# Reordering the joints of a graph-layer kernel: messages two batches ahead, weight combination in portions, first loads of the last phase on the GpSimd queue

**Chip, cores, metric.** One core of one Trainium2 chip. The metric is device microseconds for one execution; several executions of each kernel are timed and the median is given. The kernel before takes 2006.34 us (three runs, 2004.92 to 2007.96).

## The reference

A pre-norm graph layer on x of 32 x 512 x 256, fp32, with one 512 x 512 adjacency per batch. Cut to what matters:

```python
h = jnp.maximum(_layernorm(x), 0.0)
# 1. two convolutions along the nodes (1 tap, 17 taps), each with a batch norm
c = relu(_bn(_conv1d(hT, conv1_w, 0)))
x_conv = relu(_bn(_conv1d(c, conv2_w, 8)) + hT)
# 2. messages along edges, weighted by a distance of 3 features per node
s = h @ w_se.T + b_se
A = jnp.exp(-dist(s)) * adj
x_nmp = A @ relu(h @ w_msg.T + b_msg)
# 3. a GRU cell over [x_conv, x_nmp] with state h
gi = concat([x_conv, x_nmp]) @ w_ih.T + b_ih ;  gh = h @ w_hh.T + b_hh
r, z = sigmoid(...), sigmoid(...) ;  n = tanh(gi_n + r * gh_n)
out = x + (1 - z) * n + z * h
```

## The kernel before

The 32 batches go in two groups of 16, in stages one after the other:
- *first part* of a group: layer norm, transposed h, first convolution, its windows taken to frequency space. In the first group TensorE also generates the second convolution's weights there ("steps").
- *node loop* of a group: message, distances, aggregate for each batch, interleaved with *products* (the second convolution in frequency space).
- *last phase*: pairs of batches; inverse transform, then the gates by a seven-product block scheme. It needs sums of weights (the *combination*: `wraw` to `wsum7`, stored, later loaded as `sw`) and sums of the operands `hp` (h), `np` (aggregate) and `cp` (convolution).

```python
def statistics(b):                      # VectorE, then one GpSimd power
    for c in range(NC):
        nc.vector.bn_stats(...); nc.vector.bn_aggr(...)
    nc.vector.tensor_scalar(rstd, mv[:, :, 1], LN_EPS, None, op0=ALU.add)
    nc.gpsimd.tensor_tensor(rstd, rstd, minus_half[:, :NC], op=ALU.pow)

def first_part(g, xf, between):
    ...
    for b in range(b0, b1):
        if b + 3 < b1: load_x(b + 3, nc.gpsimd)
        if b == b0:    conv1(b)
        if b + 2 < b1: statistics(b + 2)
        if b + 1 < b1: transpose_h(b + 1)
        if b + 2 < b1: normalise(b + 2)
        one, two = between(b - b0)
        ... # conv1(b), steps `one`, windows_to_freq(b - 1), steps `two`

def nodes(g, xf, last):
    load_nodes(b0); message(b0); features(b0); factors(b0)
    for b in range(b0, b1):
        affinity(b)
        if more: load_nodes(b + 1); message(b + 1); features(b + 1)
        ... # two products
        if more: factors(b + 1)
        aggregate(b); save_nmp(b); HT.pop(b)
        ... # remaining products

with phase("pw"):
    with phase("nodes"): nodes(0, xf, GB)
    with phase("first", "sums"):
        combine_weights()               # all three, ahead of the second first part
        first_part(1, xf, lambda i: ([], []))
    with phase("nodes"): nodes(1, xf, GB - 3)

# last phase, all on the sync queue
load_pair(0); sw = load_combined()
sums(HP[0], True); sums(NP[0], False); inverse(0); sums(CP[0], False)
for p in range(pairs): ...
```

In the traces below each engine works through its instructions in the order of its stream (at 560.11 the power comes only after all of the combination's operations from 554.02 on). So "ahead" and "behind" in this text mean places in one engine's stream.

## Time and profile before

| | before |
|---|---|
| median | 2006.34 us |
| profiled span | 2007.6 us |
| TensorE busy / idle | 1929.0 / 78.6 us |
| largest waits of TensorE in the joints | features in the node loops 15.8, normalised x 14.1, first load of the last phase 11.6, first load of the next group 4.6 |

The lines behind this are in the prediction below. How to read a timeline line: start, duration, engine, source line, operation, out<-in, shape, how many instructions, and in brackets the engine's idle time before it with what ended that. In a waits line the three numbers are total us, times, longest. A window row has its stretch, its length, the busy time of PE, PEld, DVE, ACT and POOL, TensorE's granted clock as a share of full speed, the DMA share (mean busy share of the 16 transfer engines) and GB/s. PE is TensorE's matmuls and PEld its weight loads, DVE is VectorE, ACT ScalarE, POOL GpSimd, and SPq the sync queue. Of the tile names, phT is the transposed x, px the windows in frequency space, psl and psr belong to the features, pn is the aggregate (in the last phase a gate), yt the stored result of the second convolution, which the inverse transform (pc from yt) reads.

### The profile page before, as it was taken

What the parts mean: (1) busy time and instruction counts of PE and PEld (TensorE: products, weight loads), DVE (VectorE), ACT (ScalarE), POOL (GpSimd) and SP (SyncE); (2) the same over time, 40 slices, a digit from 0 to 9 for tenths busy, and PEclk for the clock granted to TensorE, in tenths of its full rate; (3) what the DMA queues carried; (4) which work ended last, traced back from release to release, by engine and by line L of the source; (5) the groups of instructions that cost most, each with busy time, mean ns of one, the idle gap of its engine ahead of it and who ended that gap; (6) DMA issues with size and microseconds to landing.
All of it is one profiled execution on the core that took longest, in us unless ns stands there. A gap on an engine that the chain in (4) does not pass through costs nothing.

```text
span 2007.6 us, 21238 instructions
## 1 busy us (share of the span) xinstructions
PE 1929.0 (96%) x7328; PEld 1188.8 (59%) x7328; DVE 1158.1 (58%) x2197; ACT 546.3 (27%) x930; POOL 541.7 (27%) x544
## 2 busy tenths in 40 slices
PE   7998999999799999998799999999999999999997
PEld 5666667766598677775455455554555545555453
DVE  7774666666795566664234555445554455544555
ACT  2444333333144233332122112221122212222121
POOL 2330323333521334340413221222213222132210
PEclk9997999999899999998699999999999999999998
DMA  8997788787654879884804331334213442134301
GB/s 208 289 262 210 201 234 221 229 233 211 228 194 130 223 226 241 242 222 114 263 20 123 123 86 54 107 124 123 78 53 116 124 123 76 51 121 124 123 11 53
DMA packets 238506, 310.92 MB, mean 155 GB/s; under 512 B 13775, under 2 KB 188687, under 8 KB 237631
## 3 DMA queue, kind: packets, MB, share of 16 engines
q1 hardware_dynamic: 220991, 260.72, 45.7%
q10 hardware_dynamic: 12224, 31.86, 4.1%
q0 software_dynamic: 5184, 16.98, 3.2%
q8 instruction: 59, 0.97, 0.2%
q14 instruction: 48, 0.39, 0.1%
HBM read 202.62 MB, written 106.89 MB: 154 GB/s over the span
## 4 chain that ended last, share of the span: by engine, by line
PE 87%; DVE 6%; DMA 4%; issue 2%; ACT 1%; POOL 1%; SPq 0%; DVEq 0%; POOLq 0%; ACTq 0%
PE pg L492 29%; PE pn L492 14%; PE pn L398 11%; PE py L316 9%; PE pc L481 6%; PE pm L350 6%; PE pc L269 3%; PE px L283 2%; DMA wd<-wst 2%; PE pd L384 2%; PE po L615 1%; PE pw L214 1%; DVE x L245 1%; DVE stats L234 1%; PE phT L256 1%
## 5 line engine op out<-in xcount | busy, mean ns | idle before, releaser
L398 PE MATMUL pn<-A,msg 128*128 128x512 f32 x512 | 231.5, 605 | 3.8 <-DVE A L390 3.8
L492 PE MATMUL pg<-hp,sw 128*128 128x512 f32 x448 | 229.8, 595 | 0.0
L492 PE MATMUL pg<-np,sw 128*128 128x512 f32 x448 | 229.7, 594 | 0.0
L492 PE MATMUL pg<-cp,sw 128*128 128x512 f32 x448 | 229.2, 593 | 0.0
L470 POOL TENSOR_TENSOR hp<-hp 128x512 f32<-128x512 f32 x64 | 80.5, 1268 | 476.3 <-DMA hp<-hd 268.9
L398 PEld LDWEIGHTS pn<-A,msg 128*128 128x128 f32 x512 | 96.8, 195 | 116.4 <-issue 110.1
L470 POOL TENSOR_TENSOR cp<-cp 128x512 f32<-128x512 f32 x64 | 80.5, 1268 | 296.2 <-ACT cp L486 294.9
L507 ACT ACTIVATE rz<-rz,brz 128x512 f32<-128x512 f32 x96 | 69.2, 721 | 298.7 <-DVE rz L511 298.7
L492 PEld LDWEIGHTS pg<-cp,sw 128*128 128x128 f32 x448 | 85.4, 191 | 107.7 <-issue 107.5
L492 PEld LDWEIGHTS pg<-np,sw 128*128 128x128 f32 x448 | 85.4, 191 | 107.7 <-issue 107.0
L316 PE MATMUL py<-wt,both 128*128 128x256 f32 x624 | 147.5, 379 | 0.0
L308 POOL TENSOR_TENSOR both<-xf 128x256 f32<-128x256 f32 x78 | 58.9, 755 | 301.5 <-PE py L316 256.2
L350 PEld LDWEIGHTS pm<-wmsg,hT 128*128 128x128 f32 x512 | 124.3, 327 | 25.3 <-issue 22.0
L492 PEld LDWEIGHTS pg<-hp,sw 128*128 128x128 f32 x448 | 83.0, 191 | 92.6 <-issue 89.0
L389 DVE STREAM_TRANSPOSE at<-adj 128x512 f32<-128x512 f32 x128 | 134.7, 1086 | 1.8 <-DMA adj<-in_adj_dram 1.4
L350 PE MATMUL pm<-wmsg,hT 128*128 128x259 f32 x512 | 135.4, 419 | 0.0
L481 PEld LDWEIGHTS pc<-back,yt 120*128 120x128 f32 x1024 | 123.4, 201 | 20.0 <-DMA yt<-yd 12.8
L311 POOL TENSOR_TENSOR wsum<-wt 128x512 f32<-128x512 f32 x78 | 101.6, 1302 | 124.4 <-DMA wt<-wd 120.7
L400 DVE COPY nmp<-pn 128x512 f32<-128x512 f32 x64 | 44.3, 692 | 157.5 <-PE pn L398 157.5
L481 PE MATMUL pc<-back,yt 120*128 120x80 f32 (+1 forms) x1024 | 123.2, 284 | 11.8 <-DMA yt<-yd 11.6
L316 PEld LDWEIGHTS py<-wt,both 128*128 128x128 f32 x624 | 118.9, 191 | 25.2 <-issue 10.8
L269 PE MATMUL pc<-w,hT 128*128 128x256 f32 x512 | 121.0, 391 | 0.6 <-DVE hT L257 0.6
(110 smaller groups left out, 2964.5 us busy)
## 6 DMA issues: line engine op xcount, KB each, us to landing
wt<-wd SPq DMA_DIRECT2D x160, 256.0 KB, 5.6
adj<-in_adj_dram SPq DMA_DIRECT2D x128, 256.0 KB, 5.2
yd<-y ACTq DMA_DIRECT2D x80, 384.0 KB, 5.7
yt<-yd SPq DMA_DIRECT2D x64, 480.0 KB, 10.0
wd<-wst SPq DMA_DIRECT2D x64, 320.0 KB, 5.1
x<-in_x_dram SPq DMA_DIRECT2D x38, 512.0 KB, 5.5
hd<-hT SPq DMA_DIRECT2D x32, 512.0 KB, 4.1
hT<-hd SPq DMA_DIRECT2D x32, 512.0 KB, 3.5
```

The lines of the kernel that those rows point to most:

```text
L269: nc.tensor.matmul(p[:, j, :], HT[b][:, ic, c * P : (c + 1) * P], w1[:, ic, :], start=(ic == 0), stop=(ic == DC - 1))
L308: nc.gpsimd.tensor_tensor(both[:, 0], re, im, op=ALU.add)
L311: nc.gpsimd.tensor_tensor(wsum, wr, wi, op=ALU.add)
L316: nc.tensor.matmul(dst, v[:, ic, :], w[:, ic, :], start=(ic == 0), stop=(ic == DC - 1))
L350: nc.tensor.matmul(p[:, : D + NS], chunk(HT[b][:, ic, :], c), wmsg[:, ic, :], start=(ic == 0), stop=(ic == DC - 1))
L389: nc.vector.transpose(at.rearrange("p (j k) -> p j k", k=32), ADJ[b].rearrange("p j (q c) -> p c j q", c=NC)[:, mc])
L398: nc.tensor.matmul(p, MSG[b][:, mc, dc * P : (dc + 1) * P], A[b][:, mc, :], start=(mc == 0), stop=(mc == NC - 1))
L400: nc.vector.tensor_copy(NMP[b][:, dc, :], p)
L470: nc.gpsimd.tensor_tensor(t[:, dst, :], t[:, a, :], t[:, b, :], op=sub)
L481: nc.tensor.matmul(bk[:, t0:t1], YT[p][j * W + w][:, oc * P : (oc + 1) * P], back[:, u0 : u0 + t1 - t0], start=(w == 0), stop=(w == W - 1) ...
L492: nc.tensor.matmul(bk, sw[:, k, q, o, :], terms[k][q], start=(first and i == 0), stop=(i == len(ks) - 1), skip_group_check=True)
L507: nc.scalar.activation(rz[:, g, j, :], src, AF.Sigmoid, bias=brz[:, g : g + 1], scale=1.0)
```

## The change

The intent: keep TensorE busy where one stage ends and the next starts. Five parts:
1. The generated weights' steps are spread over 15 batches instead of 16, so that their last stores are done before the node loop.
2. The node loop sends messages two batches ahead and distances one ahead. It starts with the group's last batch, whose hT is kept in SBUF.
3. The combination moves from ahead of the second first part into it, one third after each of the batches 2, 6 and 10.
4. The first loads of the last phase go out on the GpSimd queue, while the node loop still runs; yt ahead of np; the combined weights in two portions, the first-needed first (the operands are renumbered for that).
5. In the last pair two of four blends run on GpSimd, and the first batch is finished ahead of the last blend; in every pair results are stored in halves. Further, in the second group, the second batch is normalised before the first is transposed.

```diff
 # weight steps
-                mine = spread(steps, b, GB)
-                return mine[::2], mine[1::2]
+                mine = spread(steps, b, GB - 1) if b < GB - 1 else []
+                return mine[:1], mine[1:]
 # node loop (begin(i): load hT if it isn't there, message, features)
+            todo = [b1 - 1] + list(range(g * GB, b1 - 1))
+            load_adj(todo[0])
+            begin(0)
+            factors(todo[0])
+            begin(1)
+            affinity(todo[0])
+            for i, b in enumerate(todo):
+                if more:
+                    load_adj(todo[i + 1])
+                    factors(todo[i + 1])
+                for u in mine[:1]:
+                    product(pools["pw"], g, u, xf)
+                begin(i + 2)
+                if more:
+                    affinity(todo[i + 1])
 ...                                     # a product, aggregate, save, products
 # combination
-                combine_weights()
+                def between(b):
+                    if b % 4 == 2 and b // 4 < K3:
+                        combine_weights(b // 4)
+                    return [], []
 # last phase
-        load_pair(0)
-        sw = load_combined()
-        sums(HP[0], True)
-        sums(NP[0], False)
+        load_pair(0, nc.gpsimd)
+        load_combined(sw, 0, 2)         # on the GpSimd queue
+        load_combined(sw, 2, 7)
         inverse(0)
-        sums(CP[0], False)
+        for t, keep in ((HP[0], True), (NP[0], False), (CP[0], False)):
+            sums(t, keep)
 # second group of the first part
-        transpose_h(b0)
+        if g == 0:
+            transpose_h(b0)
         statistics(b0 + 1)
         normalise(b0 + 1)
+        if g > 0:
+            transpose_h(b0)
 # last pair
+        if last:
+            blend(0, 0, nc.gpsimd)
+            blend(1, 1, nc.gpsimd)
+            blend(1, 0)
+            finish(p, 0)
+            blend(0, 1)
+            finish(p, 1)
```

(Cut: buffer counts of msg 2 to 3 and A 1 to 2, hT released after the message, order of loads within a pair, half stores.)

More of the change, by code (lines that the diff above doesn't have):

```diff
@@ L273, in conv1 @@
             nc.scalar.activation(h1, h1, AF.Relu)
-        del HT[b]
+        if b % GB != GB - 1:
+            del HT[b]
     def windows_to_freq(b, xf):
@@ L322, in product, with load_adj @@
         nc.scalar.dma_start(YD[g][:, 3 * u : 3 * u + 3, :], y)
-    def load_nodes(b):
-        load_h(b)
-        ADJ[b] = pools["nodes"].tile([P, N // 32, P], FP, tag="adj", name=f"adj_{b}")
+    def load_adj(b):
+        ADJ[b] = pools["nodes"].tile([P, N // 32, P], FP, tag="adj", name=f"adj_{b}", bufs=1)
         rows = adj[b].rearrange("(j r) (g m) -> g r j m", r=32, g=4)
@@ L340, in message @@
     def message(b):
-        MSG[b] = pools["nodes"].tile([P, NC, D], FP, tag="msg", name=f"msg_{b}", bufs=2)
+        MSG[b] = pools["nodes"].tile([P, NC, D], FP, tag="msg", name=f"msg_{b}", bufs=3)
         ST[b] = pools["nodes"].tile([P, 2, NC, NS], FP, tag="st", name=f"st_{b}", bufs=2)
@@ L354, in message @@
             nc.scalar.activation(m, m, AF.Relu)
+        del HT[b]
     def features(b):
@@ L377, in affinity @@
     def affinity(b):
-        A[b] = pools["nodes"].tile([P, NC, N], FP, tag="A", name=f"A_{b}")
+        A[b] = pools["nodes"].tile([P, NC, N], FP, tag="A", name=f"A_{b}", bufs=2)
         sl, sr = SL.pop(b), SR.pop(b)
@@ L404, in save_nmp @@
         nc.sync.dma_start(ND[b], NMP.pop(b))
-    A11, A12, S4, A22, S1, S2, S3 = range(7)
+    Q1, Q6, Q2, Q7, Q5, Q4, Q3 = range(7)
     B11, B12, B21, B22 = range(4)
-    def combine_weights():
-        sources = [w_hhT, w_ihT[D:], w_ihT[:D]]
-        for k, src in enumerate(sources):
-            w = pools["sums"].tile([P, DC, G], FP, tag="wraw", name=f"wraw_{k}")
-            nc.sync.dma_start(w, src.rearrange("(c p) o -> p c o", p=P))
-            w = w.rearrange("p c (g i o) -> p c g i o", i=2, o=P)
-            a11, a21, a12, a22 = w[:, 0, :, 0], w[:, 0, :, 1], w[:, 1, :, 0], w[:, 1, :, 1]
-            t = pools["sums"].tile([P, 7, 3, P], FP, tag="wsum7", name=f"wsum7_{k}")
-            for dst, a in ((A11, a11), (A12, a12), (A22, a22)):
-                nc.gpsimd.tensor_copy(t[:, dst], a)
-            nc.gpsimd.tensor_tensor(t[:, S1], a21, a22, op=ALU.add)
-            nc.gpsimd.tensor_tensor(t[:, S2], t[:, S1], a11, op=ALU.subtract)
-            nc.gpsimd.tensor_tensor(t[:, S3], a11, a21, op=ALU.subtract)
-            nc.gpsimd.tensor_tensor(t[:, S4], a12, t[:, S2], op=ALU.subtract)
-            nc.sync.dma_start(WS[k], t)
@@ L432, in load_combined, with combine_weights @@
-    def load_combined():
-        sw = pools["sw"].tile([P, K3, 7, 3, P], FP, name="sw")
+    def combine_weights(k):
+        src = [w_hhT, w_ihT[D:], w_ihT[:D]][k]
+        w = pools["sums"].tile([P, DC, G], FP, tag="wraw", name=f"wraw_{k}")
+        nc.sync.dma_start(w, src.rearrange("(c p) o -> p c o", p=P))
+        w = w.rearrange("p c (g i o) -> p c g i o", i=2, o=P)
+        a11, a21, a12, a22 = w[:, 0, :, 0], w[:, 0, :, 1], w[:, 1, :, 0], w[:, 1, :, 1]
+        t = pools["sums"].tile([P, 7, 3, P], FP, tag="wsum7", name=f"wsum7_{k}")
+        for dst, a in ((Q1, a11), (Q2, a12), (Q4, a22)):
+            nc.gpsimd.tensor_copy(t[:, dst], a)
+        nc.gpsimd.tensor_tensor(t[:, Q5], a21, a22, op=ALU.add)
+        nc.gpsimd.tensor_tensor(t[:, Q6], t[:, Q5], a11, op=ALU.subtract)
+        nc.gpsimd.tensor_tensor(t[:, Q7], a11, a21, op=ALU.subtract)
+        nc.gpsimd.tensor_tensor(t[:, Q3], a12, t[:, Q6], op=ALU.subtract)
+        nc.sync.dma_start(WS[k], t)
@@ L434, in load_combined, with load_pair @@
+    def load_combined(sw, q0, q1):
         for k in range(K3):
-            nc.sync.dma_start(sw[:, k], WS[k])
-        return sw
-    def load_pair(p):
+            nc.gpsimd.dma_start(sw[:, k, q0:q1], WS[k][:, q0:q1])
+    def load_pair(p, queue=nc.sync):
+        NP[p] = pools["ops"].tile([P, 7, N], FP, tag="np", name=f"np_{p}")
         HP[p] = pools["ops"].tile([P, 8, N], FP, tag="hp", name=f"hp_{p}")
-        NP[p] = pools["ops"].tile([P, 7, N], FP, tag="np", name=f"np_{p}")
         YT[p] = []
@@ L443, in load_pair @@
             b = 2 * p + j
-            nc.sync.dma_start(HP[p][:, j:4:2], HD[b])
-            nc.sync.dma_start(NP[p][:, j:4:2], ND[b])
-        for j in range(2):
-            b = 2 * p + j
+            queue.dma_start(HP[p][:, j:4:2], HD[b])
             g, w0 = b // GB, (b % GB) * W
@@ L451, in load_pair @@
                 w = w0 + k * (W // 2)
-                nc.sync.dma_start(t, YD[g][w : w + W // 2].rearrange("w r d -> r w d"))
+                queue.dma_start(t, YD[g][w : w + W // 2].rearrange("w r d -> r w d"))
                 YT[p] += [t[:, i, :] for i in range(W // 2)]
+        for j in range(2):
+            queue.dma_start(NP[p][:, j:4:2], ND[2 * p + j])
     def load_pair_x(p):
@@ L463, in operands @@
         t3 = 7 if keep else B12
-        return [t[:, i, :] for i in (B11, B21, B22, 6, 4, 5, t3)]
+        return [t[:, i, :] for i in (B11, 5, B21, t3, 4, 6, B22)]
     def sums(t, keep):
@@ L493, in into @@
                              skip_group_check=True)
-    Q1, Q2, Q3, Q4, Q5, Q6, Q7 = range(7)
     def temp(role, name):
@@ L542, in gates_rz, with gate_n @@
             result(b3[o], u2[o], o, 0, 1)
-    def gate_n(p, terms):
+    def gate_n(p, terms, last):
         rz, o = RZ[p], 2
@@ L567, in closing, with blend @@
             nc.scalar.activation(n, n, AF.Tanh, bias=b_in[:, i : i + 1], scale=1.0)
-        def blend(i, j):
+        def blend(i, j, engine=nc.vector):
             n, d = nt[:, i, j, :], rz[:, i, j, :]
-            nc.vector.tensor_sub(d, HP[p][:, 2 * i + j, :], n)
-            nc.vector.tensor_mul(d, d, rz[:, DC + i, j, :])
-            nc.vector.tensor_add(n, n, d)
+            engine.tensor_tensor(d, HP[p][:, 2 * i + j, :], n, op=ALU.subtract)
+            engine.tensor_tensor(d, d, rz[:, DC + i, j, :], op=mul)
+            engine.tensor_tensor(n, n, d, op=add)
         x1 = [bank(f"pn1_{p}_{k}") for k in range(2)]
@@ L602, in gate_n @@
         closing(x3[1], 0, 1)
-        for i, j in ((0, 0), (1, 1), (1, 0), (0, 1)):
-            blend(i, j)
+        if last:
[5 more added lines that the diff above has]
+            finish(p, 1)
+        else:
+            for i, j in ((0, 0), (1, 1), (1, 0), (0, 1)):
+                blend(i, j)
     def finish(p, j):
@@ L617, in finish @@
             nc.vector.tensor_add(xo, xo, bk)
-        nc.sync.dma_start(out[b].rearrange("(c p) d -> p c d", p=P), xb)
+            nc.sync.dma_start(out[b].rearrange("(c p) d -> p c d", p=P)[:, c0 : c0 + h], xo)
     def spread(todo, i, n):
@@ L690, in nodes, with begin @@
         def nodes(g, xf, last):
-            b0, b1 = g * GB, (g + 1) * GB
+            b1 = (g + 1) * GB
+            todo = [b1 - 1] + list(range(g * GB, b1 - 1))
             units = list(range(UNITS))
-            load_nodes(b0)
-            message(b0)
-            features(b0)
-            factors(b0)
-            for b in range(b0, b1):
-                mine = spread(units, b - b0, last) if b - b0 < last else []
-                more = b + 1 < b1
-                affinity(b)
+            def begin(i):
+                if i < GB:
+                    if todo[i] not in HT:
+                        load_h(todo[i])
+                    message(todo[i])
+                    features(todo[i])
+            load_adj(todo[0])
[4 more added lines that the diff above has]
+            for i, b in enumerate(todo):
+                mine = spread(units, i, last) if i < last else []
+                more = i + 1 < GB
                 if more:
-                    load_nodes(b + 1)
-                    message(b + 1)
-                    features(b + 1)
-                for u in mine[:2]:
+                    load_adj(todo[i + 1])
+                    factors(todo[i + 1])
+                for u in mine[:1]:
                     product(pools["pw"], g, u, xf)
+                begin(i + 2)
                 if more:
-                    factors(b + 1)
+                    affinity(todo[i + 1])
+                for u in mine[1:2]:
+                    product(pools["pw"], g, u, xf)
                 aggregate(b)
                 save_nmp(b)
-                HT.pop(b)
                 for u in mine[2:]:
@@ L718, in gnn_layer @@
             with phase("first", "sums"):
-                combine_weights()
+                def between(b):
+                    if b % 4 == 2 and b // 4 < K3:
+                        combine_weights(b // 4)
+                    return [], []
                 xf = freq_tile(1)
                 with tc.manual_schedule():
-                    first_part(1, xf, lambda i: ([], []))
+                    first_part(1, xf, between)
             with phase("nodes"):
@@ L729, in gnn_layer @@
         pairs = B // 2
-        load_pair(0)
-        sw = load_combined()
-        sums(HP[0], True)
-        sums(NP[0], False)
+        sw = pools["sw"].tile([P, K3, 7, 3, P], FP, name="sw")
+        load_pair(0, nc.gpsimd)
+        load_combined(sw, 0, 2)
+        load_combined(sw, 2, 7)
         inverse(0)
-        sums(CP[0], False)
+        for t, keep in ((HP[0], True), (NP[0], False), (CP[0], False)):
+            sums(t, keep)
         for p in range(pairs):
@@ L754, in gnn_layer @@
                 sums(CP[p + 1], False)
-            gate_n(p, terms)
-        for j in range(2):
-            finish(pairs - 1, j)
+            gate_n(p, terms, not more)
 def kernel(**inputs):
```

## The prediction

> **What bounds the kernel now.** I began with the page's busy shares and its 40 slices.
>
> ```profile
> PE 1929.0 (96%) x7328; PEld 1188.8 (59%) x7328; DVE 1158.1 (58%) x2197; ACT 546.3 (27%) x930; POOL 541.7 (27%) x544
> ```
>
> TensorE bounds it: 1929.0 of 2007.6 us busy. The static comparison of the two kernels gives the same instructions and shapes on every engine, in another order. So only two things can be won: TensorE's idle time (78.6 us), and the stretching of its work at half clock. To see where they lie I cut the span by stage (columns: stretch, length, busy time of PE, PEld, DVE, ACT, POOL with instruction counts, granted clock, DMA share, GB/s).
>
> ```profile
> 0.00:150.00 150.00, 136.67 (x760) 95.09 (x760) 115.11 (x310) 64.21 (x140) 45.07 (x67) 0.99 0.93 253
> 150.00:230.00 80.00, 67.64 (x295) 48.88 (x292) 43.59 (x105) 29.74 (x58) 15.42 (x16) 0.85 0.73 206
> 230.00:500.00 270.00, 270.00 (x1079) 187.49 (x1078) 177.42 (x344) 88.47 (x146) 93.43 (x103) 1.00 0.80 224
> 500.00:540.00 40.00, 26.17 (x111) 19.63 (x110) 29.59 (x65) 4.34 (x9) 19.90 (x24) 0.79 0.67 235
> 540.00:630.00 90.00, 89.77 (x550) 83.52 (x549) 73.71 (x199) 36.30 (x86) 23.89 (x28) 1.00 0.49 172
> 630.00:680.00 50.00, 45.37 (x177) 32.22 (x177) 25.01 (x62) 16.52 (x27) 13.54 (x15) 0.93 0.68 176
> 910.00:964.00 54.00, 44.09 (x140) 25.51 (x138) 25.74 (x56) 13.85 (x22) 0.00 (x0) 0.87 0.36 93
> 964.00:992.00 28.00, 16.52 (x67) 14.91 (x68) 3.46 (x5) 2.89 (x4) 11.90 (x10) 0.55 0.98 319
> 992.00:1990.00 998.00, 998.00 (x3214) 514.62 (x3212) 505.89 (x745) 215.57 (x316) 229.05 (x183) 1.00 0.31 93
> ```
>
> The loops' steady states (230 to 500, 680 to 910) and the last phase from 992 are 100% busy at full clock: nothing to win. The loss sits in the joints. Counting idle time plus busy time x (1 - clock):
> - first part to node loop, 150 to 230: 12.4 + 10.1 = 22.5 us
> - node loop to second first part, 500 to 540: 13.8 + 5.5 = 19.3
> - second first part to second node loop, 630 to 680: 4.6 + 3.2 = 7.8
> - end of that loop, 910 to 964: 9.9 + 5.7 = 15.6
> - start of the last phase, 964 to 992: 11.5 + 7.4 = 18.9
>
> Sum 84 us. The start and the final blends (some 28 us more) are hardly touched.
>
> TensorE's waits name the causes (total, times, longest):
>
> ```profile
> PE psl L370 <- DVE fr L364: 15.8, 6, 4.1
> PE phT L256 <- DVE x L245: 14.1, 6, 6.3
> PE pc L481 <- DMA yt<-yd: 11.6, 1, 11.6
> PE px L283 <- DVE hT L257: 4.6, 1, 4.6
> ```
>
> The first is the ends of the node loop, where the chain message, features, factors, affinity of one batch has no other batch's work beside it. The other three I followed in the timeline:
>
> ```profile
> 151.01 0.43 DVE L234 BATCH_NORM_STATS2 stats<-x 128x6 f32<-128x256 f32 x1 [5.26 <-DMA x<-in_x_dram]
> 513.52 0.99 POOL L429 TENSOR_TENSOR wsum<-wraw,wsum 128x384 f32<-128x384 f32 x1
> 514.47 1.02 POOL L239 TENSOR_TENSOR rstd<-rstd,minus_half 128x4 f32<-128x4 f32 x1
> 515.52 3.19 DVE L245 TENSOR_SCALAR x<-x,mv,rstd 128x256 f32<-128x256 f32 x4 [4.91 <-POOL rstd L239]
> 543.42 1.40 POOL L425 COPY wsum<-wraw 128x384 f32<-128x384 f32 x3 [2.95 <-DMA wraw<-in_w_ihT_dram]
> 975.33 2.00 PE L481 MATMUL pc<-back,yt 120*128 120x72 f32 x8 [11.60 <-DMA yt<-yd]
> 989.49 2.01 PE L492 MATMUL pg<-hp,sw 128*128 128x512 f32 x2
> ```
>
> At 151 statistics of the next group's x, hoisted into this phase, wait for a load and hold VectorE's queue. At 514 the power that gives rstd sits behind the weight combination on GpSimd; the normalise behind it then takes 3.19 us instead of 1.4. At 975 TensorE has waited 11.6 us for the first load of the last phase.
>
> **What the Trainium skill says.** (1) "TensorE: Matmul & The Clock Gate", part 1: after an idle window of about 3.4 us the clock is halved, and it returns after a busy window of that length. The trace agrees on the fall (4.57 us idle at 150, 11.6 at 964) but not on the return: it stayed at half for about 12 us after the first and some 15 us after the second. I charge 3 to 6 us for each gap over 3 us. (2) "GPSIMD Engine Reference", section 1, Specifications: its SBUF interface is shared with VectorE. It agrees: 3.19 us against 1.4. (3) "DMA: Bandwidth & Descriptors", "Anatomy of one DMA": a semaphore wait happens on the issuing sequencer. This decides the part on the GpSimd queue; the kernel before has no such case to test it. (4) Same page, "Issuing engines are not separate DMA queues": all share the same 16 engines, so another queue brings an earlier start, not more bandwidth. From 964 the DMA share is already 0.98.
>
> **Part by part.**
>
> *First part to node loop (22.5 us lost).* The load of the next group's first x moves ahead of the store of hT, so it is issued right after the transposes it follows, about 3.8 us earlier; a second normalise (3.7 us of VectorE) is hoisted there too. Of the 4.57 us wait 0 to 2 remain, and most of the clock loss behind it goes: about 7. The generated weights' steps end one batch earlier, so the wait of the node loop's first additions on their stores (3.7 us, then 3.25 on TensorE) goes, and a second message lies in the gap of the first features: about 9. Sum 16.
>
> *Node loop to second first part (19.3 lost).* The power no longer queues behind five combine operations (509.2 to 514.5), and the second batch is normalised already. Statistics of the third are still on the path: I leave 8 us, gain 11.
>
> *Combination inside the second first part (a new cost).* It now comes after the batches 2, 6 and 10. GpSimd is in order: copies 1.40 + four operations of 0.99 = 5.3 us, a load issue 0.8, the power 1.03; and ahead of them the wait for a raw load issued only just before. Such loads took 5.1, 9.2 and 9.0 us from issue to landing. With h the end of the hT copy of one batch: issue h + 0.45, landing h + 6.5 to 9, combine to h + 12 to 14, power to h + 14, then normalise and transpose at h + 14 to 16.5. The undisturbed loop transposes next at about h + 10.3. Stall 3.7 to 6.2 us, three times, with half clock behind it (3 to 4): 8 x 3 = 24 lost (9 to 33). Before, the second and third combination stood with their input loaded, or ahead of slack: 0.23 us of TensorE.
>
> *Second first part to node loop (7.8 lost).* Two messages and two feature chains stand side by side, and the loop begins with the last batch, whose hT is still in SBUF. Gain 5.5.
>
> *End of the second node loop.* From the end of the last product (914.1) to the last aggregate (963.8) are 49.6 us, for about 34 us of TensorE work at full clock. After, one message and distance set (5 us) has been done before it; and my hand schedule of the rest ends 31.3 us after the last product, set by VectorE's transposes and products for the last two batches (4 x 1.05 + 4 x 0.65 each) and a single adjacency buffer, loaded late. 49.6 - 31.3 - 5.2 = 13.
>
> *Start of the last phase.* Loads go out on GpSimd's queue in order: h of batch 0, its first yt, then the second yt. That one waits until its memory is free, which by the placement is at the last adjacency transpose (about 26 us after the last product), and it holds everything behind it, also sums (5.2 us each). By hand: inverse from 33.7 to 40.5 us after the last product, first gate products until 46, the second set waits for the sums of the context until 51.3, ends 54.7: 23.4 us after the last aggregate. Before, the same point is 35.7 us after it (999.5). Gain 12 (7 to 14).
>
> *End.* Two of four last blends on GpSimd (3 x 1.27 each) beside VectorE's (3 x 0.69), stores in halves: gain 1.
>
> Sum: 16 + 11 - 24 + 5.5 + 13 + 12 + 1 = 34.5 us. 2006.3 - 34.5 = 1971.8; I say 1971.
>
> **Rivals.**
> 1. *The combination hides.* For it: GpSimd is only 27% busy, the second first part has the lowest DMA share of the early stages (0.49), so the raw load may land in 5 us; VectorE runs some batches ahead on x. Against: the power of the next batch is in the same in-order queue, two batches of lead at most. Then 1950 to 1957.
> 2. *The combination costs its full worth*, each stall followed by a cold clock of 12 us: 33 lost, 1980; with it the x loads of later batches, also on that queue, come late: 1985 to 1990.
> 3. *The late loads give nothing*, because the second yt blocks the GpSimd queue longer than I think (the queue also carries the issue of the combined weights) and the sums behind come last: TensorE then waits for hp or the context instead of yt, gain 0 for this part, 1984.
> 4. *DMA becomes the bound in the first part*, whose share is 0.93 and which now gets its steps in 15 batches instead of 16. Speaks for it: adding 7% to a rate of 0.93. Against: the weight steps are only a part of that traffic. It would cost up to 5.
>
> **Range and chances.** The joint gains total 58.5, give or take 12; the combination is -9 to -33, and the sum is most sensitive to it. Taken together 1955 to 1990. The 2% border is 1966.2, 5 us below my centre, with a spread of some 13: faster 0.4, same 0.58, slower 0.02.
>
> **What would show it.** Right: no wait of 4.6 us for px at 150; the transposes' 6.3 us wait at the second first part gone, and three new waits of 3 us or more there, named rstd, x or wraw, with the clock dipping in that phase (540 to 630 had 1.00); the last aggregate ending about 21 us earlier (16 + 11 - 24 + 5.5 + 13), near 942; the 11.6 us wait for yt under 4; TensorE's idle time near 60 us. Wrong: a second first part at full clock without waits means rival 1; a new wait of 8 us or more for hp, sw or yt means rival 3; a TensorE stage longer in steady state (some 20 us per batch in the node loop) would break the premise that only joints change.

## The result, and the profile after

1972.79 us median (four runs, 1971.33 to 1973.28), beside 2005.63 of the kernel before on the same chip: ratio 0.9837, interval 0.982 to 0.9855. The gain of 1.6% is clear of the noise and stays under the 2% border that the prediction names.

The page of the changed kernel, busy shares:

```profile
PE 1916.8 (97%) x7328; PEld 1185.1 (60%) x7328; DVE 1131.3 (57%) x2191; ACT 545.2 (28%) x930; POOL 570.3 (29%) x564
```

TensorE has the same 7328 instructions; idle is now 54.7 us (1971.5 - 1916.8), and its busy time shrank by 12.2 us though no work left it. This is half clock saved: by the clock records of the two traces, busy time lost to half clock fell from 37.2 to 21.2 us; that is 16.0, so some 4 us of other busy time were added, which stay unexplained. By stage (columns as before; the stages have moved earlier, so the stretches differ where needed):

```profile
150.00:230.00 80.00, 78.04 (x359) 57.33 (x358) 50.51 (x135) 33.90 (x66) 18.04 (x20) 0.98 0.81 231
500.00:540.00 40.00, 36.50 (x182) 31.43 (x183) 27.77 (x82) 10.16 (x24) 12.95 (x17) 0.88 0.55 186
540.00:630.00 90.00, 78.59 (x435) 70.43 (x434) 56.00 (x152) 29.53 (x70) 26.08 (x32) 0.92 0.44 155
630.00:680.00 50.00, 48.95 (x211) 36.24 (x211) 31.43 (x80) 19.14 (x32) 14.31 (x17) 1.00 0.77 206
890.00:940.00 50.00, 48.54 (x179) 28.57 (x177) 29.79 (x57) 13.95 (x23) 12.34 (x16) 1.00 0.56 153
940.00:970.00 30.00, 25.07 (x89) 15.55 (x88) 4.38 (x6) 5.62 (x8) 17.94 (x17) 0.83 1.04 331
```

Counted as in the prediction (idle time plus busy time x (1 - clock)), three joints are nearly closed: 150 to 230 loses 3.5 us where it lost 22.5, 630 to 680 loses 1.1 of 7.8, the end of the second node loop 1.5 of 15.6. The start of the last phase is half closed (9.2 of 18.9), and the front of the second first part somewhat more (8.3 from 484 to 524, of 19.3). But 540 to 630, which was full (89.77 of 90 at clock 1.00), now has 11.4 us of idle time and clock 0.92. TensorE's waits after:

```profile
PE phT L256 <- issue: 12.9, 3, 5.9
PE po L619 <- DVE nt L570: 9.5, 2, 6.7
PE pc L479 <- DMA yt<-yd: 4.6, 2, 2.6
PE phT L256 <- DVE x L245: 4.0, 2, 3.8
PE psl L371 <- DVE fr L365: 2.1, 2, 1.1
```

The features' wait fell from 15.8 to 2.1, that for yt from 11.6 to 4.6, the px wait is gone. At the top stand three new waits of the transposes. They are called "issue", which names nothing; the timeline of all engines around the second does ("..." marks lines left out):

```profile
547.63 0.39 SPq L421 DMA_DIRECT2D wraw<-in_w_ihT_dram  x1
...
554.02 1.40 POOL L426 COPY wsum<-wraw 128x384 f32<-128x384 f32 x3 [6.84 <-DMA wraw<-in_w_ihT_dram]
...
559.29 0.79 POOL L104 DMA_DIRECT2D x<-in_x_dram  x1
...
560.11 1.05 POOL L239 TENSOR_TENSOR rstd<-rstd,minus_half 128x4 f32<-128x4 f32 x1
...
561.19 1.45 DVE L245 TENSOR_SCALAR x<-x,mv,rstd 128x256 f32<-128x256 f32 x4 [7.86 <-POOL rstd L239]
561.70 2.32 PE L256 MATMUL phT<-ident,x 128*128 128x128 f32 x8 [5.91 <-issue]
```

GpSimd idles 6.84 us for the raw load, combines for 5.3 us, issues a load, and only then makes the power on which VectorE's normalise and TensorE's transposes wait. The hT copy ended at 547.2 (= h of the prediction); transposes at 561.7 are h + 14.5.

Where the 36.1 us of span came from, with stage bounds read from the two traces (TensorE's first instruction of a stage to the first of the next; the end of the last aggregate and of the last gate matmul for the last three). By the medians it is 32.8; the profiled run of the kernel before was one of its longer ones.

| stage | before | after | won | predicted |
|---|---|---|---|---|
| first part 1 | 184.3 | 181.2 | 3.2 | 16 with the next |
| node loop 1 | 321.9 | 309.1 | 12.8 | |
| first part 2 | 124.1 | 138.0 | -13.9 | +11 - 24 |
| node loop 2 (to the last aggregate) | 333.4 | 310.5 | 22.8 | 5.5 + 13 |
| last phase, to the last gate matmul | 1026.9 | 1015.4 | 11.5 | 12 |
| end | 17.1 | 17.3 | -0.3 | 1 |

### The profile page after: what moved, and what is told of

Read it like the earlier page. It is cut to its first block, busy times and chain, and to the rows that moved or that the text cites. A ratio compares the mean times of both kernels' runs of the same rounds, so it can differ in the third digit from the quotient of the medians.

```text
span 1971.5 us, 21287 instructions
## 1 busy us (share of the span) xinstructions
PE 1916.8 (97%) x7328; PEld 1185.1 (60%) x7328; DVE 1131.3 (57%) x2191; ACT 545.2 (28%) x930; POOL 570.3 (29%) x564
## 4 chain that ended last, share of the span: by engine, by line
PE 88%; DVE 5%; DMA 3%; issue 2%; POOL 1%; ACT 1%; SPq 0%; POOLq 0%; DVEq 0%; ACTq 0%
PE pg L490 29%; PE pn L490 14%; PE pn L399 11%; PE py L317 10%; PE pm L350 6%; PE pc L479 5%; PE pc L269 3%; PE px L284 2%; PE pd L385 2%; PE po L619 2%; PE pw L214 1%; DVE stats L234 1%; DMA wd<-wst 1%; PE phT L256 1%; DMA sw<-ws 1%
## 5 line engine op out<-in xcount | busy, mean ns | idle before, releaser
L399 PE MATMUL pn<-A,msg 128*128 128x512 f32 x512 | 225.5, 593 | 0.3 <-DVE A L391 0.3
L317 PEld LDWEIGHTS py<-wt,both 128*128 128x128 f32 x624 | 114.2, 190 | 43.9 <-issue 27.0
L312 POOL TENSOR_TENSOR wsum<-wt 128x512 f32<-128x512 f32 x78 | 106.0, 1361 | 78.9 <-DMA wt<-wd 66.6
L269 PE MATMUL pc<-w,hT 128*128 128x256 f32 x512 | 127.6, 406 | 0.6 <-DVE hT L257 0.6
L350 PE MATMUL pm<-wmsg,hT 128*128 128x259 f32 x512 | 125.6, 398 | 0.0
L479 PE MATMUL pc<-back,yt 120*128 120x80 f32 (+1 forms) x1024 | 119.2, 278 | 4.6 <-DMA yt<-yd 4.6
L490 PE MATMUL pn<-hp,sw 128*128 128x512 f32 x224 | 115.1, 595 | 0.0
```

The costliest lines, as they stand in the source:

```text
L269: nc.tensor.matmul(p[:, j, :], HT[b][:, ic, c * P : (c + 1) * P], w1[:, ic, :], start=(ic == 0), stop=(ic == DC - 1))
L312: nc.gpsimd.tensor_tensor(wsum, wr, wi, op=ALU.add)
L317: nc.tensor.matmul(dst, v[:, ic, :], w[:, ic, :], start=(ic == 0), stop=(ic == DC - 1))
L350: nc.tensor.matmul(p[:, : D + NS], chunk(HT[b][:, ic, :], c), wmsg[:, ic, :], start=(ic == 0), stop=(ic == DC - 1))
L399: nc.tensor.matmul(p, MSG[b][:, mc, dc * P : (dc + 1) * P], A[b][:, mc, :], start=(mc == 0), stop=(mc == NC - 1))
L479: nc.tensor.matmul(bk[:, t0:t1], YT[p][j * W + w][:, oc * P : (oc + 1) * P], back[:, u0 : u0 + t1 - t0], start=(w == 0), stop=(w == W - 1) ...
```

## The experiments

All kernels gave correct results. Every ratio is against the kernel before on the same chip; the changed kernel's is 0.9837. Stage lengths come from one profiled run each and scatter by some 2 us between runs (first part 1 of the changed kernel: 181.2, and 179.0 in its repeat, experiment 11).

### 1. The raw loads earlier

```diff
+    if b % 4 == 0 and b // 4 < K3:
+        load_raw(b // 4)
     if b % 4 == 2 and b // 4 < K3:
-        combine_weights(b // 4)         # load, then combine
+        combine_weights(b // 4)         # combine only
```

> The changed kernel with only the three raw weight loads issued two batches earlier (the combination itself stays after batches 2, 6 and 10). My theory: the three stalls of the second first part (2.25, 5.91 and 4.69 us of TensorE idle, named 'issue' in its waits) come from a raw load issued directly ahead of the combination; with the load landed, 5.3 us of GpSimd work fit beside the batch, each stall falls under 1 us and the second first part shortens from 138.0 to about 120 us; total about 1955 us. Rival: the 5.3 us of GpSimd work, or its sharing of SBUF with VectorE, is itself too long for the in-order queue; then stalls of 2 to 4 us remain and the total is 1965 to 1970.

Measured: 1952.81 us (1950.71 to 1955.47), ratio 0.9741 (0.9717 to 0.9765). The second first part took 117.7 us instead of 138.0. The three stalls fell to 1.14 us or less:

```profile
554.89 1.76 PE L256 MATMUL phT<-ident,x 128*128 128x128 f32 x8 [1.14 <-issue]
583.57 1.69 PE L256 MATMUL phT<-ident,x 128*128 128x128 f32 x8 [1.12 <-issue]
```

GpSimd's waits in the changed kernel, from 480 to 640 us, had these two lines; the same view of this kernel has none for the raw weights:

```profile
POOL wsum L426 <- DMA wraw<-in_w_ihT_dram: 12.5, 2, 6.8
POOL wsum L426 <- DMA wraw<-in_w_hhT_dram: 5.5, 1, 5.5
```

So 20 us hung on the wait for a load issued directly ahead of its use. The GpSimd work itself is all still there; beside it the transposes wait at most 1.14 us. The rival (the work is too long) falls.

### 2. The combination ahead of the second first part again

```diff
-    def between(b): ...                 # a third after batches 2, 6, 10
-        first_part(1, xf, between)
+    for k in range(K3):
+        combine_weights(k)
+    first_part(1, xf, lambda i: ([], []))
```

> The changed kernel with the combination put back ahead of the second first part, as in the kernel before. My theory: moving it was a net loss of 13 us (11 won at the front, 24 lost in three stalls), so undoing it gives about 1960 us: a wait of 6 us for the normalised x at the start of that part returns, the three stalls go. Rival: moving it was a gain in itself and the stalls have another cause (for instance late x loads on the GpSimd queue): then 1980 us or more, with both the front wait and stalls.

Measured: 1955.8 us (1955.79 to 1957.37), ratio 0.9757 (0.9734 to 0.978). That the change as a whole gains 1.6% hides that this part of it lost 17 us (1972.8 - 1955.8). As in the kernel before, the transposes wait at the front:

```profile
503.01 2.37 PE L256 MATMUL phT<-ident,x 128*128 128x128 f32 x8 [7.36 <-DVE x L245]
529.40 2.25 PE L256 MATMUL phT<-ident,x 128*128 128x128 f32 x8 [3.48 <-issue]
```

and from 540 to 630 TensorE is 88.95 of 90 us busy at clock 1.00 again. The rival (a gain in itself, 1980 us or more) falls. The part took 121.2 us, 3.5 more than in the first experiment, and the medians differ by 3.0. So the combination seems better placed inside the part, once its input is there; the intervals of the two ratios overlap, so this is not shown.

### 3. Weight steps over 16 batches again

```diff
-    mine = spread(steps, b, GB - 1) if b < GB - 1 else []
-    return mine[:1], mine[1:]
+    mine = spread(steps, b, GB)
+    return mine[::2], mine[1::2]
```

> The changed kernel with the weight-generating steps spread over 16 batches of the first part as before, half of them on either side. My theory: the node loop's first VectorE additions again wait for the last stores of generated weights, about 3 us of TensorE idle and the clock falls: 6 to 9 us slower, 1979 to 1982 us. Rival: the first part is bound by the DMA and gets shorter with the steps spread wider: 1970 us or less.

Measured: 1981.31 us (1978.42 to 1982.16), ratio 0.9879 (0.985 to 0.9908): 8.5 slower. Both waits of the kernel before return, not only the one I had put down to this part:

```profile
154.60 4.96 PE L284 MATMUL px<-fwd,h 128*128 128x160 f32 x16 [4.44 <-DVE hT L257]
187.62 0.42 DVE L353 TENSOR_TENSOR msg<-pm,bmsg 128x256 f32<-128x256 f32 x1 [3.66 <-DMA wd<-wst]
189.76 0.86 PE L371 MATMUL psl<-ident,fl 128*128 128x128 f32 x4 [3.25 <-DVE fr L365]
```

In this run the sync queue issues the next group's x at 139.83, behind the store of hT at 139.32; in the changed kernel it issues it at 139.16, ahead of the store at 142.37. So the earlier load too is a consequence of how the steps are placed. (The edit undoes the number of batches and the split around the convolution together.) In the traces the whole is 8.0 us longer: 1.4 in the first part (within the scatter), 3.6 in the first node loop, 1.0 in the second first part, 1.7 in the second node loop, 0.3 behind it. The 1.7 is one stretch of half clock at the end of that loop (3.41 us from 930.7); the traces of experiments 6, 9 and 10 have one there too, so it need not come from this edit. The rival, a first part bound by the DMA, falls: with the steps spread wider that part is not shorter (182.5).

### 4. The node loop of before

The node loop, and the buffer counts that belong to it, as in the kernel before; all else as changed.

```diff
-    todo = [b1 - 1] + list(range(g * GB, b1 - 1))
-    ...                                  # begin two ahead, affinity one ahead
+    load_nodes(b0); message(b0); features(b0); factors(b0)
+    ...                                  # message one ahead, affinity in its own turn
```

> The changed kernel with the node loop of the kernel before (message and distances one batch ahead, no batch kept from the first part). My theory: the two loops won 12.8 and 22.9 us in the measured kernel, of which the loop's order made most: 7 to 9 of the first, 5.5 at the start and 13 at the end of the second; so 26 to 32 us slower, 1999 to 2005 us. Rival: most of this came from the weight steps (first loop) and the late loads (second loop): then under 12 us slower, below 1985 us.

Measured: 2003.84 us (1999.07 to 2006.19), ratio 0.9992 (0.9964 to 1.002): 31 us slower, nearly all that the change gains; the rival falls. The loops took 319.5 and 336.2 us against 309.1 and 310.5. From the end of the last product to the end of the last aggregate it is 49.5 us again (922.3 to 971.8), against 30.8 in the changed kernel (908.0 to 938.8), and the old waits are back:

```profile
930.65 1.09 PE L370 MATMUL psl<-ident,fl 128*128 128x128 f32 x4 [3.21 <-DVE fr L364]
963.02 8.80 PE L398 MATMUL pn<-A,msg 128*128 128x512 f32 x16 [2.34 <-DVE A L390]
```

In this kernel some 19 us more of node loop lie between the last product and the last phase (49.5 - 30.8), in which the loads can hide, and the inverse waits only 1.0 us; so the two parts help at the same place, and their gains don't simply add. Two messages ahead, the kept batch and the buffer counts were undone together; no run tells them apart.

### 5. The late loads on the sync queue again

```diff
-        load_pair(0, nc.gpsimd)
+        load_pair(0)
-            nc.gpsimd.dma_start(sw[:, k, q0:q1], WS[k][:, q0:q1])
+            nc.sync.dma_start(sw[:, k, q0:q1], WS[k][:, q0:q1])
```

> The changed kernel with the first loads of the last phase (first pair and combined weights, in the new order and portions) on the sync queue again. My theory: the queue is what lets the first loads start before the node loop ends; on the sync queue they stand behind the last store of the loop, the inverse waits some 6 to 7 us for its first yt and the clock falls: about 7 us slower, 1980 us (the order and the portions keep 5 of the 12 us won there). Rival: order and portions made the whole gain, since all queues share the same transfer engines: 1971 to 1975 us.

Measured: 1978.24 us (1976.69 to 1979.36), ratio 0.9866 (0.9838 to 0.9894): 5.5 slower; from the last aggregate to the end of the span 1038.9 us against 1032.7, so 6.2 by the traces (1.7 of it idle time, most of the rest half clock). The inverse starts after the wait expected:

```profile
944.30 14.16 PE L479 MATMUL pc<-back,yt 120*128 120x72 f32 x64 [6.58 <-DMA yt<-yd]
```

The queue made about half of the 11.5 us won in the last phase, by starting earlier; the rival falls. The other half is left for order and portions, which no run undid alone. The transfer engines are at the same share (1.03 against 1.04 from 940 to 970), so no bandwidth was won.

### 6. The last blends on VectorE

```diff
-            blend(0, 0, nc.gpsimd)
-            blend(1, 1, nc.gpsimd)
+            blend(0, 0)
+            blend(1, 1)
```

> The changed kernel with the last pair's two GpSimd blends on VectorE again (order and half stores kept). From the trace of the changed kernel: three VectorE operations took 1.53 to 1.64 us beside GpSimd instead of 0.69 (2.8 us lost), the blends on VectorE cost 6 x 0.69 = 4.1 us: nearly a wash, 0 to 2 us slower, 1973 to 1975 us. Rival: the GpSimd blends are what made the tail 0.8 us longer than before: 2 to 3 us faster, 1970 us.

Measured: 1973.52 us (1972.93 to 1978.82), ratio 0.985 (0.9823 to 0.9876): no difference that the interval shows. In the traces the end after the last gate matmul is 18.7 us (1953.4 to 1972.1) against 17.3 (17.2 to 17.5 in the other runs). So the two blends on GpSimd win 1.4 us there: 4.1 us leave VectorE (6 x 0.69), and most of it is paid back by what GpSimd slows there, for example

```profile
1952.13 1.68 POOL L568 TENSOR_TENSOR rz<-hp,nt 128x512 f32<-128x512 f32 x1 [2.17 <-ACT nt L563]
...
1952.72 1.64 DVE L558 TENSOR_TENSOR nt<-nt,p_n 128x512 f32<-128x512 f32 x1
```

in the changed kernel, where the same VectorE addition alone takes 0.69.

Without GpSimd's help the new end is 1.6 us longer than that of the kernel before (17.1), and the order shows where. The last eight transposes start 10.2 us after the last gate matmul in the kernel before (first line, 1990.6) and 12.7 after it in this run (last line, 1953.4), as the first batch's closing additions now stand ahead of the last blend on VectorE:

```profile
2000.83 1.97 PE L615 MATMUL po<-ident,nt 128*128 128x128 f32 x8 [0.30 <-DVE nt L574]
1962.49 0.69 DVE L621 TENSOR_TENSOR x<-x,po 128x512 f32<-128x512 f32 x1 [0.99 <-PE po L619]
1963.95 0.68 DVE L568 TENSOR_TENSOR rz<-hp,nt 128x512 f32<-128x512 f32 x1
1966.14 1.97 PE L619 MATMUL po<-ident,nt 128*128 128x128 f32 x8 [2.83 <-DVE nt L570]
```

Behind the last addition the half stores end 0.9 us sooner (3.2 instead of 4.1). This is read from the traces; no run undid order or half stores alone.

### 7. The order of transposes and second normalise as before

```diff
-        if g == 0:
-            transpose_h(b0)
+        transpose_h(b0)
         statistics(b0 + 1)
         normalise(b0 + 1)
-        if g > 0:
-            transpose_h(b0)
```

> The changed kernel with the transposes of a group's first batch ahead of the second batch's statistics and normalise in both groups, as before. My theory: the second normalise (about 3.7 us of VectorE with its statistics) then lies between the first node loop and the second first part: 2 to 4 us slower, 1975 to 1977 us. Rival: it is hidden there anyway and was only a load on VectorE at the end of the first part: 1970 to 1973 us.

Measured: 1972.43 us (1970.7 to 1973.99), ratio 0.9838 (0.9814 to 0.9862): no difference; my theory falls. The stage bounds suggest where it goes: the first part of the first group ends at 176.9 (178.5 to 181.2 in the other runs with 15 batches of steps), and the second first part takes 140.4 (136.6 to 138.0 in the other runs with its three stalls, but for 139.0 in experiment 3). So the work was moved from one joint to another, by little more than the scatter, and nothing was won.

### 8. The second pair's loads later

```diff
-                load_pair(p + 1)
+                load_pair(p + 1, nc.sync if p > 0 else nc.gpsimd)   # behind the first pair's sums
```

> The changed kernel with the loads of the second pair on the GpSimd queue behind the sums of the first pair, so that 4 MB less compete with the first pair's yt and combined weights (DMA share 1.04 from 940 to 970). Theory: TensorE's two waits for yt (2.6 and 2.0 us) and the slow clock there are bandwidth; they shrink, 3 to 5 us faster, 1968 to 1970 us. Rival: they are the late start of the loads (held back by the memory of the last adjacency tile), and the bandwidth does not matter: 1972 to 1974 us.

Measured: 1971.12 us (1970.11 to 1972.29), ratio 0.9834 (0.9806 to 0.9861): no difference. The waits for yt went from 2.60 and 2.00 to 2.04 and 1.63 us. The DMA share from 940 to 970 did fall, from 1.04 to 0.91, so my theory (bandwidth) falls: the contention with the next pair is not what these waits hang on. That the start of the loads counts is what experiment 5 shows.

### 9 to 11. A better version, beside the changed kernel

To experiment 1 was added, for the second group only, that the third batch's statistics go ahead of the first batch's shift additions on VectorE; the tenth run also has experiment 8; the eleventh is the changed kernel once more.

```diff
+            if b == b0 and g > 0:
+                statistics(b + 2)
             if b == b0:
                 conv1(b)
-            if b + 2 < b1:
+            if b + 2 < b1 and (b > b0 or g == 0):
                 statistics(b + 2)
```

> The changed kernel with the raw loads two batches earlier (as in the first experiment) and, in the second first part, the third batch's statistics ahead of the first batch's shift additions on VectorE. Theory: the remaining wait of the transposes at the start of that part (3.8 us on the normalised x) comes from those statistics starting 3.9 us after the previous copies; placed earlier, the wait falls to about 1 us and the clock dips less: 3 to 5 us faster than the first experiment, 1948 to 1950 us. Rival: the wait moves on to the next batch, as VectorE and TensorE are nearly balanced there: 1952 to 1954 us.

> The same with the second pair's loads behind the first pair's sums on the GpSimd queue too. That move alone gave 0.03% which is no difference; expected here 0 to 1 us faster than the run before it. If it is over 3 us faster, contention between the two pairs' loads matters after all.

> The changed kernel as it stands, repeated on this chip beside the two others, so that they can be compared with it and not only with the kernel before: 1971 to 1975 us, ratio 0.9837 within 0.002.

Measured: 1951.82 us, ratio 0.9731 (0.9708 to 0.9754); 1950.46 us, 0.9724 (0.9703 to 0.9745); 1972.79 us, 0.9838 (0.9815 to 0.9862). The changed kernel repeats. The wait at the front fell from 3.80 to 1.43 us and the part took 114.4 us, 3.3 less than in experiment 1:

```profile
495.62 1.73 PE L256 MATMUL phT<-ident,x 128*128 128x128 f32 x8 [1.43 <-DVE x L245]
```

yet the medians differ by 1.0 us only and the intervals overlap, so whether the earlier statistics help the whole is open. (Part of the 3.3 went again in the second node loop, 312.3 against 310.5, to one stretch of half clock near its end.) The tenth run shows no difference to the ninth. What stands is that these versions take about 21 us less than the changed kernel and 2.7% less than the one before, and that experiment 1 makes nearly all of it.

## Why the prediction was right

The time (1971 predicted, 1972.79 measured) was right, and the sum by joints mostly for its reasons. That it came within 2 us is luck: single terms missed by up to 4 us, in both directions. Step by step:

- *First part to node loop, 16 expected, 16.0 measured by stages* (3.2 + 12.8). The sum was right, its split was not, and by the prediction's own count the joint won 19 (22.5 lost before, 3.5 after). I gave 7 us to an earlier x load and a hoisted normalise, and 9 to the weight steps and a second message. Experiment 3 gives about 5 us of these stages to the steps, including the x load (3.6 of it clear of the scatter); experiment 4 gives 10.4 us of the first node loop to its order; experiment 7 gives the hoisted normalise nothing in the total.
- *Node loop to second first part, 11 expected, about 11 measured.* From the part's start to 34 us on (before) or 33 us on (changed kernel, 523, ahead of the first stall) TensorE lost 17.9 us to idle time and half clock before, 7.1 after. The second batch's normalise, which I counted in, was by experiment 7 only moved.
- *Combination, 24 expected, 20 to 22 measured.* The mechanism was right in every link: raw load just ahead, GpSimd in order, power behind it, transposes at h + 14.5 where I had h + 14 to 16.5. The stalls were 2.25, 5.91 and 4.69 us where I had 3.7 to 6.2. The half clock behind them was oversized: in windows of 2 us it cost 1.7, 3.0 and 2.5 us, I had charged 3 to 4. So 12.9 of idle time and 7.1 of clock; experiment 1, without the stalls, is shorter by 20.3 in this part (138.0 - 117.7). The rest of the part's loss is short waits (1.9) and some 3 us of TensorE's busy time that this count does not explain. Together: -13 expected, -13.9 measured.
- *Second node loop, 18.5 expected, 22.8 measured.* The end went as the hand schedule said: 30.8 us from the last product to the last aggregate, 31.3 expected. The start won more: from 630 to 680 TensorE is now idle for 1.05 us at clock 1.00, so 6.7 of the 7.8 lost, where I had 5.5. Of the 22.8, 11.8 are idle time and 9.1 half clock (six times 3.41 us before, none after); 1.9 are busy time that this count does not explain.
- *Start of the last phase, 12 expected, 11.5 measured.* The chain on the GpSimd queue was as worked out: the second yt held back by VectorE's last adjacency transpose, and everything behind it:

```profile
933.90 0.79 POOL L448 DMA_DIRECT2D yt<-yd  x1 [21.22 <-DVE at L390]
934.69 0.73 POOL L443 DMA_DIRECT2D hp<-hd  x1
```

  That is 25.9 us after the last product (908.0), where I had "about 26". I had the stall at the wrong operand: no gate product waited for the context's sums; TensorE waited 2.60 and 2.00 us for the second batch's yt instead, and the clock was at half until about 957. The inverse ran from 30.6 to 45.5 us after the last product, where I had 33.7 to 40.5, and the first gate product started at 45.8. That the total still fits (11.5 for 12) is in part luck.
- *End, 1 expected, -0.3 measured*: GpSimd's help is worth 1.4 us by the traces of experiment 6; it is lost to the new order, in which the last blend waits behind the first batch's closing additions.

Of the rivals, the hidden combination is what experiment 1 builds: I said 1950 to 1957 for it, and 1952.8 came. The full cost (33 us, a cold clock of 12 us behind each stall) did not come: the half clock behind the stalls lasted 3.4, 6.8 and 6.8 us. The others (blocked GpSimd queue without gain, DMA-bound first part) are refuted by experiments 5 and 3. Not settled: the 2 to 3 us of busy time left over in the second first part and the second node loop, and the later 3 us of experiment 3.

Of the signs named in advance, the px wait and the 6.3 us wait of the transposes went (3.8 is left), the yt waits stayed under 4 (2.60 at most), idle time is 54.7 for "near 60" and the last aggregate ends at 938.8 for "near 942". One sign failed in part: only two of the three stalls are over 3 us, and the profile names none of them. Three readings in the prediction were off: the half clock before lasted 13.7 us from 154.2 (I read about 12) and, behind the 11.6 us wait, 18.5 us from the restart of work at 975.3 (I read some 15); and not every engine keeps its instructions, as six blend operations move from VectorE (2197 to 2191) to GpSimd.

## What to carry to other kernels

A small operation that is needed each round (here one power for rstd) makes its in-order engine part of the critical path, however idle that engine is on average: never put work behind a fresh load into that stream, issue the load a round or two earlier. Total time can hide this: the change gained 33 us in spite of a part that lost 17, and only undoing the parts one at a time showed it. A wait that is named "issue" should be followed by the timeline of all engines; one step of another engine's queue explained it.

## What the Trainium skill lacked or had wrong

- "TensorE: Matmul & The Clock Gate", part 1, has the clock halve after an idle window of about 3.4 us and return after a busy one of that length, and calls the window free-running. The clock records of the traces fit a free-running window: between the start and the end of a run, every stretch of half clock of all 13 traces lasts a whole number of times 3.41 us (one to eight). But the runs show a fall 2.8 us after idle time began (592.1 to 594.9 in the changed kernel), so a window of 3.41 us with 0.6 us of work in it was enough. And one busy window did not always bring the clock back: after the stalls it returned with the first window full of work (526.63 to 530.05, 560.77 to 567.59, 594.90 to 601.73), but in the kernel before it stayed at half from 966.55 to 993.86 though TensorE was busy for 14.52 of the 15 us from 975 to 990 with the inverse. Why is open. In the repeat (experiment 11) the second stall, 5.59 us, cost one such stretch and not two, so some 1.7 us hang on where the window falls; a charge of 2 to 3 us per gap in this loop fitted better than my 3 to 4.
- "GPSIMD Engine Reference", section 1, Specifications, names the shared SBUF interface but no size in that section (other pages of the skill say more on the sharing). Runs: a VectorE operation with two SBUF inputs took 1.53 to 1.64 us beside GpSimd instead of 0.69, GpSimd's own 1.60 to 1.81 instead of 1.27, and a group of normalises, an operation with one tensor input, 2.60 instead of 1.45 (experiment 1, at 538).
- "DMA: Bandwidth & Descriptors", "Anatomy of one DMA": that the wait is on the issuing sequencer is confirmed (21.22 us on the GpSimd queue before one yt load, all others behind it). "Issuing engines are not separate DMA queues" is confirmed too, with the size of the earlier start: 6 us of 1972, at the same DMA share. What "Anatomy of one DMA" lacks is the cost of a load among others: its fit of a fixed part plus a size part gives about 3.1 us for 480 KB and 2.9 for 384 KB (estimates from the page); with the share at 1.04 the 480 KB loads took 7.5 us and the 384 KB portions 16.2 (medians, issue to landing).
